# Start of a conditional residual layer: batch 0's input alone, bf16 parts on two engines, row picks dealt out among the first products, beta added first

## The chip, the cores and the metric

The kernel runs on one core of one Trainium2 chip. The core has five engines that work side by side, each through its own instructions in order: TensorE (PE in the profile, its weight loads PEld), VectorE (DVE), ScalarE (ACT), GpSimd (POOL) and SyncE (SP), which here only issues transfers (DMAs). On-chip memory is SBUF, and PSUM for the products of TensorE. Times are device microseconds of one execution; the kernel before took 308.53 us (median of three runs, 308.47 to 308.71).

## The reference

For each of 128 batches (x is [128, 128, 512]: batch, row, column) a language id picks one of 10 small adapters (the setup makes 10 languages; ids are 0 to 8):

```python
w1 = W1[language_ids]                                   # [512, 128] per batch
w2 = W2[language_ids]                                   # [128, 512]
h = relu(einsum('bsh,bha->bsa', x, w1) + b1[language_ids])
adapted = einsum('bsa,bah->bsh', h, w2) + b2[language_ids]
y = x + adapted
normed = (y - mean(y)) * rsqrt(var(y) + 1e-5)           # over the 512 columns
out = x + normed * gamma[language_ids] + beta[language_ids]
```

All of it is float32.

## The kernel before

**Tables.** The rows of beta, gamma and b2 (10 each, 30 in all) are needed on all 128 partitions. They are loaded once as 30 rows (`rows`), split into three bf16 parts whose sum is the float32 value (`parts`, at partitions 0, 32 and 64), and each row is spread by one TensorE product with a column of `pick` (`spread`, L201 to L211): the product selects the three parts of one row, adds them and repeats the sum on all partitions. VectorE or ScalarE copies it from PSUM to one of the tables `beta_b`, `gamma_b`, `b2_b` in SBUF; a row r goes to ScalarE where r % 7 is 1, 3 or 5. `spread_turn(lo, hi)` spreads rows lo to hi - 1: 0 to 9 are beta, 10 to 19 gamma (stored as -gamma/2), 20 to 29 b2. A later use takes the row by a register that holds the batch's language id, so it waits until all ten rows of that table are there. The registers are loaded four batches at a time (`lid`).

**One batch.** TensorE transposes x in four 128x128 pieces (`transpose_x`), ScalarE copies them to SBUF (`copy_xT`); TensorE makes the down product in eight matmuls (`down`), ScalarE adds b1 and applies the relu (`relu`), TensorE makes the up product (`up`). b2 comes in by one of three ways: GpSimd adds the row to x beforehand into a tile r (`add_b2`), VectorE adds it to the product (`vector_b2`), or TensorE adds it as one more bf16 product (inside `up`). The functions `b2_by_matmul` and `b2_by_vector` choose. VectorE then adds the residual and takes row sums (`residual`), ScalarE squares with row sums (`square`) and takes the root, VectorE refines it in three short steps (`rstd`), scales by gamma (`scale`) and writes the result onto the output tile (`finish`). GpSimd has filled that tile with x + beta before (`add_beta`). SyncE stores two batches at a time (`store`).

**Order.** Every instruction is kept in the written order on its engine (`keep`). After the start, a loop over i does for batch i the transposes, for i - 1 the down product, for i - 2 the up product, and for b = i - 3 VectorE's part. In turn b GpSimd adds b2 of batch b + 2, then beta of batch b. There are 5 output tiles of two batches, 4 tiles r, 4 tiles of x (four batches each) and 5 PSUM tiles for products, which the spread rows use too; who fills a tile again waits for its last reader, and a fifth-next output tile so waits for the store of the one before it. Up to batch 8, W1 of a batch is loaded from memory; from 9 on ScalarE copies it out of a table of all ten (`stage_w1`), first `w1e`, loaded at the start in two transfers.

**The start** loads, in SyncE's order: ids, gamma, x of batches 0 and 1, W2 of languages 0 to 2, then W1 of single batches, x two batches at a time, the rest of W2, and `w1e`; ScalarE's queue loads beta, b2, b1. x of batches 10 and 11 is the last of the list, the next four batches of x follow. TensorE first runs `spin`: products of a tile of ones that nothing uses. Then come batches 0 to 3 up to their relu, with the 30 rows spread in between, and the first two up products. The loop begins with i = 3.

**The end.** The last four batches run through `tail`, where GpSimd takes over part of the work of 123, 124 and a quarter of 125 (`by_pool`), and where the stores of 124 and 125 are issued by ScalarE.

Of the kernel before, what the change touches and what calls it, by code (L numbers as in the profile page):

```python
# [8 lines left out]
FP = mybir.dt.float32  # L9
BF = mybir.dt.bfloat16  # L10
I32 = mybir.dt.int32
AF = mybir.ActivationFunctionType
ALU = mybir.AluOpType
ET = mybir.EngineType
PSUM = bass.MemoryType.PSUM

P = 128
# [5 lines left out]
U = 2  # L23
# [3 lines left out]
def cond_resid_kernel(ctx: ExitStack, tc: tile.TileContext, x, itok, W1, b1, W2, b2, gamma, beta, out):  # L27
# [8 lines left out]
    nc = tc.nc  # L36
    B, S, H = x.shape
# [8 lines left out]
    def keep(ins):  # L46

        engine = ins.ins.engine
        if engine in last:
            tc.add_manual_dep(ins.ins, last[engine], behind, reason="kept order")  # L50
        last[engine] = ins.ins.name
        return ins
# [14 lines left out]
    E = B - 5  # L67
# [19 lines left out]
    def load_part(lo, hi):  # L87
        dst = xs[lo // G][:, lo % G : lo % G + hi - lo, :]
        keep(nc.sync.dma_start(out=dst, in_=x[lo:hi].rearrange("b s h -> s b h")))
# [2 lines left out]
    keep(nc.scalar.dma_start(out=rows[0:L, :], in_=beta))  # L92
    keep(nc.sync.dma_start(out=rows[L : 2 * L, :], in_=gamma))
    keep(nc.scalar.dma_start(out=rows[2 * L : 3 * L, :], in_=b2))
    load_part(0, 2)
    keep(nc.scalar.dma_start(out=b1r, in_=b1))

    warm = const.tile([P, 1], FP, name="warm")
# [2 lines left out]
    def load_w1(k):  # L101
        keep(
            nc.sync.dma_start(out=w1[:, :, k, :], in_=W1[:, k * P : (k + 1) * P, :].rearrange("l p a -> p l a"))
        )

    ident = const.tile([P, P], FP, name="ident")
    make_identity(nc, ident)
    eps = const.tile([P, 1], FP, name="eps")
    nc.gpsimd.memset(eps, EPS)
    ones = const.tile([P, P], BF, name="ones")  # L110
    nc.gpsimd.memset(ones, 1.0)

    R = 3 * L
# [64 lines left out]
    load_early(5, L)  # L180
    load_part(2 * G + 2, 3 * G)

    left = rp.tile([P, H], FP, tag="r", name="left")
    keep(nc.vector.tensor_copy(parts[0:R, :], rows[0:R, :]))
    keep(nc.vector.tensor_tensor(left[32 : 32 + R, :], rows[0:R, :], parts[0:R, :], ALU.subtract))
    keep(nc.vector.tensor_copy(parts[32 : 32 + R, :], left[32 : 32 + R, :]))
    keep(nc.vector.tensor_tensor(left[64 : 64 + R, :], left[32 : 32 + R, :], parts[32 : 32 + R, :], ALU.subtract))
    keep(nc.vector.tensor_copy(parts[64 : 64 + R, :], left[64 : 64 + R, :]))

    b1T = const.tile([P, L], FP, name="b1T")  # L190

# [23 lines left out]


    def b2_by_matmul(b):
        return b in (5, B - 1)

    def b2_by_vector(b):  # L220
        return b < 4 or 8 <= b < B - 8 and (b % 4 == 1 if b < 24 else b % 16 in (1, 6, 11) or b % 32 == 30)

    def stage_w1(b):
        w1s[b] = wp.tile([P, KC, A], FP, tag="w1s", name=f"w1s_{b}")
# [22 lines left out]
    def add_beta(b):  # L247
        g, j = divmod(b, 2)
        if j == 0:
            os[g] = op.tile([P, 2, H], FP, tag="o", name=f"o_{g}")  # L250
        v = lid(b, ET.Pool)
        keep(nc.gpsimd.tensor_tensor(os[g][:, j, :], xb(b), beta_b[:, bass.ds(v * H, H)], ALU.add))  # L252

    def down(b):
        phs[b] = p_h.tile([P, P], FP, tag="h", name=f"ph_{b}")
        for k in range(KC):
            keep(
                nc.tensor.matmul(  # L258
                    phs[b], lhsT=w1s[b][:, k, :], rhs=xT[b][:, k, :], start=(k == 0), stop=(k == KC - 1)
                )  # L260
            )
        del xT[b], w1s[b]
# [5 lines left out]
    def up(b):  # L268
        v = lid(b, ET.PE)
        ys[b] = p_y.tile([P, H], FP, tag="y", name=f"py_{b}")  # L270
        m = b2_by_matmul(b)
        if m:
            pick_b = pick[:, bass.ds(v + 2 * L, 1)].to_broadcast([96, P])
            keep(nc.tensor.matmul(ys[b], lhsT=pick_b, rhs=parts[:96, :], start=True, stop=False))
        keep(nc.tensor.matmul(ys[b], lhsT=hT[b], rhs=w2[:, bass.ds(v * H, H)], start=not m, stop=True))  # L275
        del hT[b]
# [203 lines left out]
    def spin(n, width):  # L480
        idle = p_s.tile([P, H], FP, tag="s", name="idle")
        for _ in range(n):
            keep(
                nc.tensor.matmul(
                    idle[:, :width], lhsT=ones, rhs=ones[:, 0:1].to_broadcast([P, width]), start=True, stop=True
                )
            )


    spin(9, H)  # L490
    spin(1, H // 2)

    def spread_turn(lo, hi):
        for r in range(lo, hi):
            spread(r, nc.scalar if r % 7 in (1, 3, 5) else nc.vector)

    def x_turn(b):
        transpose_x(b)
        copy_xT(b)

    x_turn(0)
    transpose_b1()
    spread_turn(0, 4)
    x_turn(1)
    spread_turn(4, 11)
    down(0)
    relu(0)
    spread_turn(11, 15)
    down(1)
    relu(1)  # L510
    x_turn(2)
    spread_turn(15, 19)
    x_turn(3)
    down(2)
    relu(2)
    spread_turn(19, 24)
    down(3)
    relu(3)
    spread_turn(24, R)
    up(0)  # L520
    up(1)

    for i in range(3, B + U):
        b = i - U - 1
        if b > G and b % G == 2 and b // G + 3 < NG:
            load_x(b // G + 3)
        if i == 5:
            load_x(3)
        if i in (8, 10, 12, 14):
            load_w1((i - 8) // 2)  # L530
        if i == 4:
            up(2)
        if i == 5:
            up(3)
        if i > 3 and on(i):
            transpose_x(i)
        if b <= E:
            add_b2(b + 2)
            add_beta(b)
        if i > 4 and on(i - 1):  # L540
            down(i - 1)
        if i > 3 and on(i):
            copy_xT(i)
        if b == 2:
            scalar_means(0)
            deviation(0)
        if i > 4 and on(i - 1):
            relu(i - 1)
        if i + 1 >= LATE and on(i + 1):
            stage_w1(i + 1)  # L550
        if i > 5 and on(i - U):
            up(i - U)


        g, half = divmod(b, 2)
        p = g - 1
        mine, old = 0 <= p < B // 2, 0 <= p - 1 < B // 2
        if b == E:
            add_b2(b + 3)
            add_beta(b + 1)  # L560
            add_b2(b + 4)
            for n in range(b + 2, B):
                add_beta(n)
        if b > E:
            tail(b)
        elif half == 0:
            if on(b):
                vector_b2(b)
                residual(b)
                square(b)  # L570
            if mine:
                scale(2 * p)
                rstd(p, 1)
            if old:
                finish(2 * p - 1)
                store(p - 1)
        else:
            if on(b):
                vector_b2(b)
            if mine:  # L580
                rstd(p, 2)
            if on(b):
                residual(b)
                square(b)
            if mine:
                rstd(p, 3)
                scale(2 * p + 1)
            if mine:
                finish(2 * p)
        if 0 < g and b <= E and half == 1:  # L590
            scalar_means(g)
            deviation(g)
        if FIRST <= i + 1 < LATE:
            stage_w1(i + 1)

        for n, engine in ((i + 3, ET.Activation), (i - U + 3, ET.PE), (b + 1, ET.DVE), (b + 5, ET.Pool)):
            if on(n):
                lid(n, engine)

# [36 lines left out]
```

## Time and profile before

| | |
|---|---|
| runs | 308.47, 308.53, 308.71 us; median 308.53 |
| profiled execution | span 306.5 us from its first to its last instruction; the profile gives no other time for it |
| between span and median | 2.0 us |
| mean time of a beta add, a b2 add on GpSimd (128x512) | 1.395, 1.399 us, one starting each 1.23 us |
| copy of a spread row, VectorE, ScalarE | 0.68, 0.59 us |
| b2 add on VectorE | 0.70 us |
| transfers, mean over the span | 254 GB/s, 77.85 MB |

How to read the rows below. A row of the timeline gives start, duration, engine, line, operation, tiles (out<-in), shapes, how many in a row were merged, and in square brackets the idle time of the engine before it and what ended it. Busy times of merged instructions overlap: an instruction starts up to 0.1 us before the one ahead of it is recorded as ended, so the step from start to start is what one costs. Matmuls are pipelined, and their ends are modelled. A row of the waits gives engine, tile and line, who ended the wait, total, times, longest. A row of the windows gives the stretch, its length, busy time and count of each engine in the order PE, PEld, DVE, ACT, POOL, then the granted clock, the share of the DMA engines and GB/s. SPq and ACTq are the sequencers of those engines, where transfers are issued.

### The profile page before, as it was taken

Reading aid. Unit: us, or ns where it says so; the run is one execution under the profiler, and the core shown is the slowest. Engines: PE = TensorE matmul, PEld = TensorE weight load, DVE = VectorE, ACT = ScalarE, POOL = GpSimd, SP = SyncE. Lnnn points to the kernel's source line nnn. Section 1 sums busy time; section 2 is a strip of 40 time slices with the busy share of each in tenths; the row PEclk is TensorE's granted clock in tenths of the full one; section 3 lists DMA queues with packets and bytes.
Section 4 is the critical chain, followed back from the end, with each engine's and each line's share of the span. In section 5 each row is a group of like instructions: output and inputs, shape, how many; then the busy total and the mean of one; then the engine's idle time right before and its main releaser. Section 6 shows DMA issues by size and latency. Waiting matters only on the chain. (4 is left out here: it accounts for less than half of the span.)

```text
span 306.5 us, 6981 instructions
## 1 busy us (share of the span) xinstructions
PE 294.6 (96%) x1835; PEld 220.0 (72%) x1835; DVE 295.9 (97%) x771; ACT 282.3 (92%) x777; POOL 283.9 (93%) x238
## 2 busy tenths in 40 slices
PE   8999999999999999999999999999999999999960
PEld 3748787777777777777777777777777777777730
DVE  6889999999999999999999999999999999999985
ACT  3858999999999999999999999999999999999981
POOL 1349899999999999999999999999999999999994
PEclk9999999999999999999999999999999999999995
DMA  6999999976678766766777666767776666773324
GB/s 231 379 390 388 373 371 354 387 231 240 221 255 276 250 202 241 226 257 219 259 276 243 213 209 238 265 224 260 275 238 206 226 231 242 246 266 137 135 109 171
DMA packets 43769, 77.85 MB, mean 254 GB/s; under 512 B 1961, under 2 KB 7348, under 8 KB 43730
## 3 DMA queue, kind: packets, MB, share of 16 engines
q1 hardware_dynamic: 43382, 76.84, 72.1%
q10 hardware_dynamic: 348, 0.57, 0.5%
q8 instruction: 15, 0.25, 0.3%
q14 instruction: 24, 0.20, 0.2%
HBM read 43.85 MB, written 33.55 MB: 253 GB/s over the span
## 5 line engine op out<-in xcount | busy, mean ns | idle before, releaser
L252 POOL TENSOR_TENSOR o<-x,beta_b 128x512 f32<-128x512 f32 x128 | 173.9, 1395 | 10.2 <-DVE beta_b L211 9.5
L245 POOL TENSOR_TENSOR r<-x,b_b 128x512 f32<-128x512 f32 x97 | 135.7, 1399 | 7.3 <-DVE b_b L211 6.2
L258 PE MATMUL ph<-xT,w1s 128*128 128x128 f32 x1024 | 135.4, 275 | 0.0
L275 PE MATMUL py<-w,hT 128*128 x256 | 131.2, 595 | 0.5 <-DVE b_b L211 0.5
L258 PEld LDWEIGHTS ph<-xT,w1s 128*128 128x128 f32 x1024 | 124.9, 192 | 1.0 <-ACT hT L266 0.5
L235 PEld LDWEIGHTS pxT<-ident,x 128*128 128x128 f32 x512 | 66.6, 151 | 65.3 <-issue 49.2
L358 DVE SCALAR_TENSOR_TENSOR py<-py,nmean,gamma_b 128x512 f32<-128x512 f32 x126 | 95.0, 754 | 0.9 <-ACT sq L399 0.8
L367 DVE SCALAR_TENSOR_TENSOR o<-py,rstd,o 128x512 f32<-128x512 f32 x122 | 91.2, 748 | 0.0
L315 ACT ACTIVATE sq<-py,sum 128x512 f32<-128x512 f32 x124 | 85.9, 693 | 2.8 <-DVE py L292 2.5
L235 PE MATMUL pxT<-ident,x 128*128 128x128 f32 x512 | 78.2, 276 | 0.0
L239 ACT COPY xT<-pxT 128x512 f32<-128x512 f32 x128 | 74.7, 584 | 3.5 <-PE pxT L235 3.5
L292 DVE SCALAR_TENSOR_TENSOR py<-py,r 128x512 f32<-128x512 f32 x97 | 67.0, 691 | 0.2
L226 ACT COPY w1s<-w 128x512 f32 x107 | 65.5, 612 | 0.0
L266 ACT ACTIVATE hT<-ph,b1T 128x128 f32<-128x128 f32 x128 | 46.9, 366 | 7.9 <-PE ph L258 2.6
L275 PEld LDWEIGHTS py<-w,hT 128*128 128x128 f32 x256 | 39.1, 192 | 2.9 <-issue 1.0
L315 ACT ACTIVATION_READ_ACCUMULATOR sq<-py,sum 128x1 f32 x124 | 25.0, 202 | 0.0
L292 DVE SCALAR_TENSOR_TENSOR py<-py,x 128x512 f32<-128x512 f32 x31 | 21.7, 699 | 0.4
L285 DVE TENSOR_TENSOR py<-py,b_b 128x512 f32<-128x512 f32 x29 | 20.2, 695 | 0.7 <-PE py L275 0.6
L325 ACT ACTIVATE root<-ssq,eps 128x2 f32<-128x2 f32 x62 | 16.4, 265 | 0.0
L292 DVE DVE_READ_ACCUMULATOR py<-py,r 128x1 f32 x97 | 13.7, 141 | 0.0
L306 ACT ACTIVATE nmean<-sum 128x2 f32<-128x2 f32 x62 | 12.3, 198 | 0.0
L329 DVE SCALAR_TENSOR_TENSOR part<-ssq,root 128x2 f32<-128x2 f32 x62 | 9.3, 151 | 0.2 <-ACT root L325 0.2
(55 smaller groups left out, 90.4 us busy)
## 6 DMA issues: line engine op xcount, KB each, us to landing
out_dram<-o SPq DMA_DIRECT2D x61, 512.0 KB, 3.4
x<-in_x_dram SPq DMA_DIRECT2D x29, 1024.0 KB, 6.2
x<-in_x_dram SPq DMA_DIRECT2D x6, 512.0 KB, 8.8
w1e<-in_L_cond_W_dram SPq DMA_DIRECT2D x2, 1280.0 KB, 12.3
w<-in_L_cond_W_dram SPq DMA_DIRECT2D x4, 640.0 KB, 8.1
w1s<-in_L_cond_W_dram SPq DMA_DIRECT2D x9, 256.0 KB, 8.4
w<-in_L_cond_W_dram SPq DMA_DIRECT2D x1, 1792.0 KB, 10.3
w<-in_L_cond_W_dram SPq DMA_DIRECT2D x1, 768.0 KB, 5.4
```

The lines of the kernel that those rows point to most:

```text
L226: keep(nc.scalar.copy(w1s[b].rearrange("p k a -> p (k a)"), src))
L235: keep(nc.tensor.transpose(pxs[b][:, k, :], cols, ident))
L239: keep(nc.scalar.copy(xT[b], pxs.pop(b)))
L245: keep(nc.gpsimd.tensor_tensor(rs[b], xb(b), b2_b[:, bass.ds(v * H, H)], ALU.add))
L252: keep(nc.gpsimd.tensor_tensor(os[g][:, j, :], xb(b), beta_b[:, bass.ds(v * H, H)], ALU.add))
L258: nc.tensor.matmul(phs[b], lhsT=w1s[b][:, k, :], rhs=xT[b][:, k, :], start=(k == 0), stop=(k == KC - 1))
L266: keep(nc.scalar.activation(hT[b], phs.pop(b), AF.Relu, bias=b1T[:, bass.ds(lid(b, ET.Activation), 1)]))
L275: keep(nc.tensor.matmul(ys[b], lhsT=hT[b], rhs=w2[:, bass.ds(v * H, H)], start=not m, stop=True))
L292: nc.vector.scalar_tensor_tensor(ys[b], ys[b], 1.0, r, ALU.mult, ALU.add, accum_out=col(sums, b))
L315: nc.scalar.activation(sq, ys[b], AF.Square, bias=col(sums, b), scale=-float(H), accum_out=col(ssqs, b))
L358: nc.vector.scalar_tensor_tensor(ys[b], ys[b], col(nmeans, b), gamma_b[:, bass.ds(v * H, H)], ALU.add, ALU.mult)
L367: nc.vector.scalar_tensor_tensor(o, ys.pop(b), rstds[g][:, j : j + 1], o, ALU.mult, ALU.add)
```

## The change

Five things change, all but one in the start.

- x of batches 0 and 1 is loaded as two transfers instead of one.
- The tile of ones is filled before the identity matrix; the spin ahead of the first transposes is six products of 512 columns instead of nine and one of 256, and one more product follows b1's transpose.
- The bf16 parts are taken by reading the upper half of each float32 (a view of every second bf16) instead of by casts. VectorE makes two subtractions, ScalarE two copies; the third part is written by the second subtraction. The tile `left` is gone.
- The rows are spread in smaller turns among the first products (5, 3, 3, 3, 3, 3, 4 and 6 rows instead of 4, 7, 4, 4, 5 and 6), and batch 2's transposes come before the second down product.
- GpSimd adds beta of batches 0 to 3 as soon as the beta rows are spread, and in turn b it adds b2, then beta, both of batch b + 2. For batches 0 to 3, b2 is added by GpSimd (0, 2) and TensorE (1, 3) instead of VectorE. GpSimd's ids are loaded one batch further ahead.

```diff
-    load_part(0, 2)
+    load_part(0, 1)
+    load_part(1, 2)
...
+    ones = const.tile([P, P], BF, name="ones")
+    nc.gpsimd.memset(ones, 1.0)
     ident = const.tile([P, P], FP, name="ident")
     make_identity(nc, ident)
     eps = const.tile([P, 1], FP, name="eps")
     nc.gpsimd.memset(eps, EPS)
-    ones = const.tile([P, P], BF, name="ones")
-    nc.gpsimd.memset(ones, 1.0)
...
-    left = rp.tile([P, H], FP, tag="r", name="left")
-    keep(nc.vector.tensor_copy(parts[0:R, :], rows[0:R, :]))
-    keep(nc.vector.tensor_tensor(left[32 : 32 + R, :], rows[0:R, :], parts[0:R, :], ALU.subtract))
-    keep(nc.vector.tensor_copy(parts[32 : 32 + R, :], left[32 : 32 + R, :]))
-    keep(nc.vector.tensor_tensor(left[64 : 64 + R, :], left[32 : 32 + R, :], parts[32 : 32 + R, :], ALU.subtract))
-    keep(nc.vector.tensor_copy(parts[64 : 64 + R, :], left[64 : 64 + R, :]))
+    def upper(lo):
+
+        return rows[lo : lo + R, :].bitcast(BF)[:, 1 : 2 * H : 2]
+
+    keep(nc.vector.tensor_tensor(rows[32 : 32 + R, :], rows[0:R, :], upper(0), ALU.subtract))
+    keep(nc.scalar.copy(parts[0:R, :], upper(0)))
+    keep(nc.vector.tensor_tensor(parts[64 : 64 + R, :], rows[32 : 32 + R, :], upper(32), ALU.subtract))
+    keep(nc.scalar.copy(parts[32 : 32 + R, :], upper(32)))
...
     def b2_by_matmul(b):
-        return b in (5, B - 1)
+        return b in (1, 3, 5, B - 1)

     def b2_by_vector(b):
-        return b < 4 or 8 <= b < B - 8 and (b % 4 == 1 if b < 24 else b % 16 in (1, 6, 11) or b % 32 == 30)
+        return 8 <= b < B - 8 and (b % 4 == 1 if b < 24 else b % 16 in (1, 6, 11) or b % 32 == 30)
...
-    spin(9, H)
-    spin(1, H // 2)
+    spin(6, H)
...
     x_turn(0)
     transpose_b1()
-    spread_turn(0, 4)
+    spin(1, H)
+    spread_turn(0, 5)
     x_turn(1)
-    spread_turn(4, 11)
+    spread_turn(5, 8)
     down(0)
     relu(0)
-    spread_turn(11, 15)
+    spread_turn(8, 11)
+    x_turn(2)
+    for n in range(4):
+        add_beta(n)
+    spread_turn(11, 14)
     down(1)
     relu(1)
-    x_turn(2)
-    spread_turn(15, 19)
+    spread_turn(14, 17)
     x_turn(3)
+    spread_turn(17, 20)
     down(2)
     relu(2)
-    spread_turn(19, 24)
+    spread_turn(20, 24)
     down(3)
     relu(3)
     spread_turn(24, R)
+    add_b2(0)
     up(0)
     up(1)
...
         if b <= E:
             add_b2(b + 2)
-            add_beta(b)
+            if 4 <= b + 2 <= E:
+                add_beta(b + 2)
...
-        for n, engine in ((i + 3, ET.Activation), (i - U + 3, ET.PE), (b + 1, ET.DVE), (b + 5, ET.Pool)):
+        for n, engine in ((i + 3, ET.Activation), (i - U + 3, ET.PE), (b + 1, ET.DVE), (b + 6, ET.Pool)):
```

E is 123, the batch whose turn hands over to the tail.

## The prediction

> **What bounds the kernel now.** I read the page first: its busy shares say which engines could be the bound.
>
> ```profile
> PE 294.6 (96%) x1835; PEld 220.0 (72%) x1835; DVE 295.9 (97%) x771; ACT 282.3 (92%) x777; POOL 283.9 (93%) x238
> ```
>
> Four engines are nearly full, so the shares decide nothing; what matters is where each can still wait. The list of waits, for GpSimd (POOL; microseconds, times, longest):
>
> ```profile
> POOL o L252 <- DVE beta_b L211: 9.5, 1, 9.5
> POOL r L245 <- DVE b_b L211: 6.2, 1, 6.2
> POOL r L245 <- DMA x<-in_x_dram: 1.1, 1, 1.1
> POOL o L252 <- DMA out_dram<-o: 0.5, 1, 0.5
> ```
>
> All its waits lie early: for the spread rows (until 10.98, and 13.48 to 19.67), then for an x load and for a store. From about 52 us it runs to the end without a gap, an add every 1.23 us. TensorE, from 24.5 us on, also runs without a gap, 2.22 and later 2.19 us per batch.
>
> Third, the windows, because the early waits name transfers. The columns after the counts in brackets are granted clock, DMA share and GB/s.
>
> ```profile
> 23.00:33.00 10.00, 10.00 (x69) 8.45 (x69) 9.83 (x27) 8.82 (x26) 9.03 (x8) 1.00 1.05 386
> 43.00:53.00 10.00, 10.00 (x68) 8.11 (x68) 10.00 (x29) 9.70 (x27) 9.35 (x9) 1.00 1.07 355
> ```
>
> The DMA engines are full, and they stay so until about 62 us. Up to there a transfer lands by the bytes in front of it, not by when it is issued. The timeline shows whom that holds. GpSimd:
>
> ```profile
> 33.17 1.28 POOL L245 TENSOR_TENSOR r<-x,b_b 128x512 f32<-128x512 f32 x1 [1.14 <-DMA x<-in_x_dram]
> ...
> 43.19 1.27 POOL L252 TENSOR_TENSOR o<-x,beta_b 128x512 f32<-128x512 f32 x1
> ...
> 50.59 1.30 POOL L245 TENSOR_TENSOR r<-x,b_b 128x512 f32<-128x512 f32 x1
> 52.43 1.27 POOL L252 TENSOR_TENSOR o<-x,beta_b 128x512 f32<-128x512 f32 x1 [0.54 <-DMA out_dram<-o]
> ```
>
> These are the b2 add of batch 10 (waits for x of 10 and 11), the beta adds of 12 and 16 and, between, the b2 add of 18. Beta of 16 needs the output buffer that the store of batches 6 and 7 frees, and waits for that store. TensorE at the same place:
>
> ```profile
> 32.94 1.02 PE L275 MATMUL py<-w,hT 128*128 x2
> 33.80 0.63 PE L235 MATMUL pxT<-ident,x 128*128 128x128 f32 x4
> ```
>
> The second line transposes batch 10: it starts 0.63 us after GpSimd was released by the very load that it needs. Then the start, TensorE and VectorE (DVE):
>
> ```profile
> 1.19 4.45 PE L484 MATMUL idle<-ones 128*128 128x512 bf16 x10 [1.19 <-POOL ones L111]
> ...
> 6.58 1.04 PE L206 MATMUL row<-parts,pick 96*128 96x512 bf16 x4
> ...
> 17.01 1.48 PE L206 MATMUL row<-parts,pick 96*128 96x512 bf16 x6
> ```
>
> ```profile
> 3.13 0.41 DVE L184 CAST parts<-rows 30x512 bf16<-30x512 f32 x1 [0.33 <-DMA rows<-in_L_cond_b_dram]
> ...
> 5.46 0.42 DVE L188 CAST parts<-left 30x512 bf16<-30x512 f32 x1
> ```
>
> The reader sees a start of 18.3 us in which TensorE hardly idles, and parts ready at 5.88. Last the end, GpSimd, then the time to landing of the last stores:
>
> ```profile
> 291.43 5.13 POOL L252 TENSOR_TENSOR o<-x,beta_b 128x512 f32<-128x512 f32 x4
> ...
> 300.43 1.68 POOL L417 TENSOR_TENSOR o<-n,o 128x512 f32<-128x512 f32 x2
> ```
>
> ```profile
> DMA to landing us min/median/max: 2.0/2.0/2.3
> ```
>
> Two chains end here. VectorE's: last piece done at 303.04, its store issued at 303.1, landed 2.3 later at 305.4. GpSimd's: done at 302.10, ScalarE (ACT) issues that store at 302.2; it lands at 304.2 to 304.5 by these durations, 304.7 by the semaphore marks of the trace. So GpSimd's chain has a cover of 0.7 to 1.2 us.
>
> The sum goes against this execution: span 306.5. The median, 308.53, is 2.0 more, which lies outside the span and is kept.
>
> **The change part by part.**
>
> *x of batch 0 alone.* One more SP issue, 0.41 (the 2-batch issue's row). SP issues W2 from 1.96 to 2.43 and then waits for the language ids until 3.55, so 1.1 us of waiting hide it; without that cover the first W1 would land 0.4 later, still ahead of its use. At the 210 to 354 GB/s of the windows from 2 to 6 us, 0.26 MB less is 0.7 to 1.2 us: x of batch 0 is there at about 4.2 instead of by 5.1.
>
> *Ones first, shorter spin.* Spin starts at 1.0 (memset 0.75 + 0.20); six at 0.43 end at 3.6. Batch 0's transposes start at 4.2, four at the 0.21 of this stage, then b1 (0.2), one spin (0.43): first row pick at about 5.7 against 6.58, so −0.9.
>
> *bf16 parts.* Out: three casts of 0.42 on VectorE. In: two copies on ScalarE. VectorE ends at 3.13 + 2 × 0.70 = 4.5. A ScalarE copy of 30x512 is bounded by its rows of 128x128 (0.37) and 128x512 (0.61); I take 0.59, the same length. ScalarE is free at 3.61: ready at 4.8. The subtraction that reads every second bf16 is not in the trace: between a cast's 0.42 and two passes, 1.36; 0.68 taken. At the upper end, parts come at about 6.0 and the first pick 0.3 later than I say; at the lower, nothing moves. ScalarE's copies lie in its idle 2.9 us before 6.52; behind them waits only batch 0's transposed copy.
>
> *Row picks dealt finely.* No pick is removed. TensorE's work from first pick to last is 30 × 0.22 + 4 × 0.89 + 3 × 0.47 = 11.6 us, and the start took 11.75. Finer dealing can win 0.2 there. First picks at the slow pace (0.43) may cost 0.6 of the 0.9. Last pick's end: 17.5 to 17.8 instead of 18.33, last copy (now 19.53) 18.2 to 18.6.
>
> *b2 of batches 0 to 3.* VectorE loses four adds of 0.70 (−2.8). TensorE gains two products of 0.22 (batches 1, 3), GpSimd two adds of 1.23 (0, 2).
>
> *TensorE up to batch 10.* 33.80 − 0.9 (first pick) + 0.44 − 0.46 (the wait before the first up product, for row copies) = 32.9, or 33.4 with slow picks. But x of 10 and 11 lands where it did, behind the same bytes: not before 33.17, the instant GpSimd was released. So **TensorE gains at most 0.63**, whatever the start gives. ScalarE says the same: its copy of W1 for batch 9 (32.20) needs the W1 load that lies 0.52 MB ahead of that x, 1.4 us at 386 GB/s, so about 31.7. With TensorE full from there on, its end and VectorE's end are 0.4 to 0.63 earlier; I take 0.6.
>
> *GpSimd: beta first.* Four beta adds now fill the old idle time (10 to 15 us): free. Afterwards beta of n follows b2 of n, where it followed b2 of n+2. At 52.43 the gate is unchanged, the store of 6 and 7. Before, b2 was done up to 18 by then; now b2 of 18 stands behind beta of 16 and 17. What remains is the same beta adds and **one b2 add more: +1.23**. That the adds reach this gate: b2 of 10 at 33.17, then beta of 10 needs the store of 0 and 1, which stands behind 1.0 MB of x; with its own 0.52 MB that is 33.0 + 4.1 = 37.1. Behind that new wait stands b2 of 11, which VectorE's residual needs at 42.6: 3 us to spare. From there beta 10, b2 11, beta 11, b2 12 end at 42.0; beta of 12 waits until 43.19 as now; seven adds on, 51.84; wait until 52.43. So how early the spread ends does not reach GpSimd's end at all. If the windows' small DMA dips (near 47 us, 0.90 and 1.00 share) fill up, the gate moves 0.3 down. The later b2 adds lead their residual by less: by 5.0 to 7.6 us now, 3.7 less with the new order and 0.6 less with TensorE's gain; the least, batch 124, keeps about 0.1 to 0.3. VectorE need not wait.
>
> *Smaller.* POOL loads ids one batch further ahead (0.32 on its sequencer), beside running adds: nothing.
>
> **Sum.** GpSimd's end 302.10 + 1.23 = 303.33, store issued 303.4, landed 305.4 to 305.9. VectorE's end lands at 304.8. So the end moves by 0.0 to +0.5 from 305.4; I take +0.4, by the trace's marks, and 306.9 for the span: **308.9 us**, +0.1%. One measurement of this kernel cannot tell 0.2% (0.6 us) from nothing.
>
> **The rivals.**
> *A, GpSimd is not behind.* If the gate at 52.43 comes at least 0.6 earlier, or GpSimd's tail adds overlap other waits, TensorE's gain shows: −0.6, 307.9. For it: 0.6 us of slack in front of that gate. Against: the same bytes stand in front.
> *B, no cover at the end (slower).* Place: ScalarE's last store. If that landing already ends the span beside VectorE's, the whole add counts: +1.23, 309.8. It decides against me once the cover is under 0.6. For it: the marks give 0.7, my lowest bound. Against: 1.2 by the store rows.
> *C, the array stays slow longer.* Picks before 6.4 run at 0.43. If the pause between the spin and x (3.6 to 4.2) starts the count anew, fast pace comes as long after 4.2 as it now comes after 1.19 (4.9 us): 9.1 instead of 6.4, 1.3 us lost, batch 10's transposes at 34.2, GpSimd still last. At 1.7 lost the end is +0.7, 309.2; if twice that, 310.9. The profile's clock row reads full through the whole start and cannot tell. The Trainium skill (TensorE: Matmul & The Clock Gate, section on what is actually happening) has the array throttled to half speed until a free-running window of about 3.4 us was busy; by that page a pause that spoils one window would cost an estimated 1.7 us, which this trace neither shows nor excludes.
>
> **How the numbers follow.** Forecast 0.42; A 0.20 (mostly just past 0.2% faster); B 0.28; C 0.10, slower. So faster 0.20, same 0.42, slower 0.38. The forecast's own range is 308.5 to 309.1; with A and B it is 307.8 to 309.9, C's worse half left out.
>
> **What would show it.** In the profile after: first pick before 6, last row copy near 18.4; the transposes of batch 10 at about 33.2 with idle time put down to the x load; GpSimd's wait for stores grown from 0.5 to about 4 us, beta of 16 again near 52.4, its last add near 303.3; ACT's last store issue near 303.4. Wrong would be: beta of 16 well before 52 (A), GpSimd's last add in place but the span 1.2 longer (B), picks 0.43 apart past 7 us (C), or VectorE waiting for b2 adds in the middle, which I priced at nothing.

## The result, and the profile after

The changed kernel took 311.20 us (median of four, 310.23 to 311.71), the kernel before 308.60 beside it: ratio 1.0081, 95% interval 1.0060 to 1.0102. It is slower by 2.6 us, outside the predicted range of 307.8 to 309.9. The profiled execution took 311.0 us with a span of 309.2 (306.5 before): 2.7 us to explain.

The page's busy shares of the changed kernel, then rows of its list of waits:

```profile
PE 295.8 (96%) x1834; PEld 220.6 (71%) x1834; DVE 292.6 (95%) x764; ACT 283.3 (92%) x779; POOL 286.5 (93%) x240
```

```profile
POOL o L255 <- DVE beta_b L214: 11.0, 1, 11.0
POOL r L248 <- DVE b_b L214: 3.9, 1, 3.9
...
POOL o L255 <- DMA out_dram<-o: 3.2, 3, 1.2
...
PE pxT L238 <- DMA x<-in_x_dram: 0.9, 2, 0.6
...
PEld ph L261 <- DMA w1s<-in_L_cond_W_dram: 0.6, 1, 0.6
```

The shares are as they were. But transfers now end more of the waits: GpSimd's for stores grew from one of 0.5 us to three of 3.2, and TensorE waits for x and for W1. The windows say which transfers are late. First the kernel before from 4 to 8 us (the last three columns are granted clock, DMA share and GB/s):

```profile
4.00:6.00 2.00, 1.94 (x7) 0.96 (x6) 1.78 (x4) 0.00 (x0) 0.00 (x0) 1.00 1.00 354
6.00:8.00 2.00, 2.00 (x13) 1.26 (x12) 1.16 (x3) 1.36 (x3) 0.00 (x0) 1.00 1.02 380
```

The same windows of the changed kernel:

```profile
4.00:6.00 2.00, 1.69 (x7) 1.09 (x8) 0.82 (x2) 1.26 (x3) 0.00 (x0) 1.00 0.79 173
6.00:8.00 2.00, 2.00 (x6) 0.78 (x5) 1.22 (x2) 0.72 (x3) 0.00 (x0) 1.00 0.90 268
```

And its later windows, which the prediction showed of before:

```profile
23.00:33.00 10.00, 10.00 (x63) 7.97 (x62) 8.30 (x25) 8.12 (x23) 10.00 (x9) 1.00 1.05 387
43.00:53.00 10.00, 10.00 (x65) 7.89 (x65) 10.00 (x27) 9.71 (x30) 8.91 (x8) 1.00 1.06 341
```

From 4 to 8 us the kernel before moved 2 x (354 + 380) kB = 1.47 MB, the changed one 2 x (173 + 268) = 0.88 MB. The missing 0.59 MB is 1.5 us at 387 GB/s. In this stretch most packets of 2 KB still took 0.084 us, but of the 431 that began here 22 took 0.3 us or more, up to 1.39 us (2 of 715 before, up to 0.36). So parts of the loads fell behind. A load of this size leaves sixteen completion marks in the trace; those of W2's first three languages run from 6.74 to 9.25, where before they ran from 6.80 to 7.35. Afterwards the engines are as full as before, and so nothing is made up. By the trace's semaphore marks W1 of batch 0 landed at 9.94 (8.02 before), x of batches 2 and 3 at 11.97 (10.03), x of 10 and 11 at 34.45 (33.03), and the store of batches 6 and 7 ended at 54.20 (52.36). That last delay is 0.4 us more than that of x of 10 and 11, so not all of it comes from the first 8 us.

The chain that ended last, in order of time (start, duration, what), has one of these on it:

```profile
4.53 7.44 DMA x<-in_x_dram
12.11 0.72 PE pxT L238 x4
```

That is x of batches 2 and 3, from issue to landing. The chain then follows TensorE up to 284.6 us. But behind 54.26 GpSimd waits for nothing, so its own end is counted from there. TensorE's timeline, the start and batch 10:

```profile
1.01 2.74 PE L487 MATMUL idle<-ones 128*128 128x512 bf16 x6 [1.01 <-POOL ones L108]
4.31 1.10 PE L238 MATMUL pxT<-ident,x 128*128 128x128 f32 x4 [0.56 <-DMA x<-in_x_dram]
...
5.94 2.34 PE L209 MATMUL row<-parts,pick 96*128 96x512 bf16 x5
...
12.11 0.72 PE L238 MATMUL pxT<-ident,x 128*128 128x128 f32 x4 [0.32 <-DMA x<-in_x_dram]
...
18.62 1.47 PE L209 MATMUL row<-parts,pick 96*128 96x512 bf16 x6
...
35.69 0.63 PE L238 MATMUL pxT<-ident,x 128*128 128x128 f32 x4
```

The first pick is 0.64 us earlier than before, and the last six are 1.61 us later (17.01). Batch 10's transposes are 1.89 us later (33.80), and this distance then stays: TensorE is full, so what is lost at the start is lost at the end. VectorE follows TensorE; its last pieces start 1.85 us later.

GpSimd's timeline in the changed kernel, at its three waits for stores:

```profile
38.57 1.27 POOL L255 TENSOR_TENSOR o<-x,beta_b 128x512 f32<-128x512 f32 x1 [1.22 <-DMA out_dram<-o]
...
44.64 2.52 POOL L255 TENSOR_TENSOR o<-x,beta_b 128x512 f32<-128x512 f32 x2 [1.09 <-DMA out_dram<-o]
...
54.26 2.52 POOL L255 TENSOR_TENSOR o<-x,beta_b 128x512 f32<-128x512 f32 x2 [0.93 <-DMA out_dram<-o]
```

And at the end:

```profile
294.72 5.04 POOL L255 TENSOR_TENSOR o<-x,beta_b 128x512 f32<-128x512 f32 x4
...
303.63 1.68 POOL L420 TENSOR_TENSOR o<-n,o 128x512 f32<-128x512 f32 x2
```

Beta of 16 comes 1.83 us later (52.43 before), and GpSimd ends at 305.31, 3.20 later: 1.83 from the gate, 1.37 behind it.

### The profile page after: what moved, and what is told of

It is laid out like the page before. It is cut to its first block, busy times and chain, and to the rows that moved or that the text cites. A ratio compares the mean times of both kernels' runs of the same rounds, so it can differ in the third digit from the quotient of the medians.

```text
span 309.2 us, 7001 instructions
## 1 busy us (share of the span) xinstructions
PE 295.8 (96%) x1834; PEld 220.6 (71%) x1834; DVE 292.6 (95%) x764; ACT 283.3 (92%) x779; POOL 286.5 (93%) x240
## 4 chain that ended last, share of the span: by engine, by line
PE 88%; POOL 5%; DMA 2%; DVE 2%; SPq 1%; issue 1%; POOLq 0%; DVEq 0%
PE ph L261 35%; PE py L278 34%; PE pxT L238 18%; DMA x<-in_x_dram 2%; POOL o L255 2%; POOL r L248 1%; PE row L209 1%; POOL n L418 1%; DVE py L361 1%; POOL o L420 1%; DVE b_b L214 0%; POOLq L640 0%; DVE py L295 0%; SPq L155 0%; SPq L89 0%
## 5 line engine op out<-in xcount | busy, mean ns | idle before, releaser
L255 POOL TENSOR_TENSOR o<-x,beta_b 128x512 f32<-128x512 f32 x128 | 163.3, 1290 | 14.2 <-DVE beta_b L214 11.0
L248 POOL TENSOR_TENSOR r<-x,b_b 128x512 f32<-128x512 f32 x99 | 127.4, 1290 | 3.9 <-DVE b_b L214 3.9
L295 DVE SCALAR_TENSOR_TENSOR py<-py,r 128x512 f32<-128x512 f32 x99 | 68.3, 690 | 2.0 <-POOL r L248 1.6
L295 DVE SCALAR_TENSOR_TENSOR py<-py,x 128x512 f32<-128x512 f32 x29 | 20.3, 700 | 0.3
L288 DVE TENSOR_TENSOR py<-py,b_b 128x512 f32<-128x512 f32 x25 | 17.2, 690 | 0.1
```

What stands on the lines that cost most here:

```text
L248: keep(nc.gpsimd.tensor_tensor(rs[b], xb(b), b2_b[:, bass.ds(v * H, H)], ALU.add))
L295: nc.vector.scalar_tensor_tensor(ys[b], ys[b], 1.0, r, ALU.mult, ALU.add, accum_out=col(sums, b))
```

## The experiments

All runs at a glance. "TensorE" is batch 20's transposes against the kernel before; "gate" is the start of beta of 16; the next column is the time from there to the end of GpSimd's last add. These three and the span are of the profiled execution; median and ratio are of the timed runs, the ratio to the kernel before on the same chip.

| kernel | median us | ratio, 95% interval | span | TensorE | gate | gate to end |
|---|---|---|---|---|---|---|
| before | 308.53 | | 306.5 | 0 | 52.43 | 249.68 |
| changed | 311.20 | 1.0081 (1.0060 to 1.0102) | 309.2 | +1.89 | 54.26 | 251.05 |
| e1 changed, again | 311.47 | 1.0097 (1.0074 to 1.0119) | 309.8 | +3.15 | 54.68 | 250.96 |
| e2 x pair restored | 310.04 | 1.0049 (1.0026 to 1.0072) | 308.6 | +1.25 | 53.58 | 250.88 |
| e3 long spin | 310.64 | 1.0072 (1.0053 to 1.0092) | 308.9 | +1.61 | 53.93 | 250.85 |
| e4 beta behind b2 of n+2 | 310.04 | 1.0052 (1.0029 to 1.0075) | 308.1 | +1.64 | 54.23 | 249.65 |
| e5 before, x split | 309.80 | 1.0040 (1.0025 to 1.0055) | 307.0 | +0.46 | 53.15 | 249.65 |
| e6 before, GpSimd's order | 309.33 | 1.0014 (0.9999 to 1.0028) | 307.6 | -0.47 | 52.98 | 251.02 |
| e7 e2 + e3 + e4 | 308.67 | 0.9996 (0.9983 to 1.0009) | 306.8 | -0.07 | 52.75 | 249.83 |
| e8 changed, x of 1 later | 309.66 | 1.0033 (1.0019 to 1.0047) | 307.6 | +1.19 | 52.09 | 251.06 |
| e9 e8, spin, e4 | 309.03 | 1.0017 (1.0001 to 1.0033) | 307.0 | +0.52 | 53.10 | 249.75 |
| e10 before, x of 1 later | 309.15 | 1.0024 (1.0005 to 1.0044) | 307.8 | +0.60 | 54.04 | 249.75 |
| e11 before, two queues | 308.35 | 0.9990 (0.9977 to 1.0002) | 306.7 | +0.23 | 52.87 | 249.60 |
| e12 before, row halves | 310.20 | 1.0055 (1.0036 to 1.0074) | 308.3 | +2.02 | 53.63 | 249.82 |
| e13 changed, two queues | 310.89 | 1.0074 (1.0048 to 1.0100) | 309.9 | +3.44 | 54.34 | 250.91 |
| e14 e13, spin, e4 | 309.77 | 1.0039 (1.0010 to 1.0067) | 308.9 | +2.70 | 54.24 | 249.89 |
| e15 e14, b1 first | 308.40 | 0.9995 (0.9986 to 1.0004) | 306.6 | +0.10 | 52.69 | 249.76 |

The last column falls into two groups. Wherever GpSimd has the new order it is 250.85 to 251.06, wherever it has the old one 249.60 to 249.89, whatever else is changed. That is the one b2 add (1.23 us) of the prediction.

**e1, the changed kernel once more.** No edit. Is the slow start chance?

> The changed kernel once more, to see whether what its profile shows is there each time. In the profiled execution the 2 KB packets between 4.5 and 8 us took 0.4 to 1.4 us instead of 0.08, W2's first three languages landed at 9.25 (before 7.35), and every later transfer of the start came 1.4 to 1.9 late; the picks ran at 0.43 until about 9; GpSimd's beta of 16 began at 54.26 (before 52.43). Theory D (slow transfers come with the change): again 115 to 270 GB/s from 4.5 to 7, beta of 16 at 54.0 or later, 310 to 312 us. Rival N (a disturbance of that one execution): the early transfers run at 360 GB/s or more, beta of 16 near 52.5, about 309.2 us.

It is not chance: 205 and 312 GB/s in the two windows from 4 to 8 us, beta of 16 at 54.68, 311.47 us. But another thing differed, in TensorE's timeline:

```profile
5.47 1.25 PE L209 MATMUL row<-parts,pick 96*128 96x512 bf16 x5
...
9.94 1.16 PE L261 MATMUL ph<-xT,w1s 128*128 128x128 f32 x8 [2.10 <-DMA w1s<-in_L_cond_W_dram]
```

The same program ran its picks 0.22 apart here and 0.43 apart above. The fast picks won nothing: TensorE then stood 2.10 us for W1 of batch 0.

**e2, the x pair in one load again.**

```diff
-    load_part(0, 1)
-    load_part(1, 2)
+    load_part(0, 2)
```

> x of batches 0 and 1 in one transfer again, all else as changed. Theory D1 (the split x brings the slow transfers): 360 GB/s or more from 4.5 on, W2's first part landed by 7.5, beta of 16 at 52.4 to 52.6, GpSimd's last add 1.8 earlier than in the changed kernel, 309.0 to 309.5 us. Rival D2 (the split has no part in it): slow packets as in the changed kernel, beta of 16 at 54 or later, within 0.5 us of the changed kernel.

The early transfers were back at 343 and 382 GB/s, W1 of batch 0 landed at 7.99, and 1.2 us of the 2.6 were gone. (The intervals of e2 and of the changed kernel overlap; e5 and e8 below are clearer.) Still there were GpSimd's add and slow picks, behind a pause of 1.45 us. TensorE's timeline of e2:

```profile
5.20 1.10 PE L237 MATMUL pxT<-ident,x 128*128 128x128 f32 x4 [1.45 <-DMA x<-in_x_dram]
...
6.83 2.23 PE L208 MATMUL row<-parts,pick 96*128 96x512 bf16 x5
```

But beta of 16 did not come back to 52.4 to 52.6, nor the time to 309.0 to 309.5: the gate is at 53.58. VectorE finished batch 7 at 44.53 (43.27 before), the store of 6 and 7 was issued at 44.82 (44.35) and was under way for 8.7 us (8.0). Around 48 us some transfers are slow again; the windows from 47 to 50 us, of the kernel before, the changed one and e2:

```profile
47.00:50.00 3.00, 3.00 (x21) 2.40 (x20) 3.00 (x8) 2.86 (x7) 3.00 (x3) 1.00 0.98 326
47.00:50.00 3.00, 3.00 (x23) 2.53 (x22) 3.00 (x9) 3.00 (x11) 3.00 (x4) 1.00 1.03 302
47.00:50.00 3.00, 3.00 (x22) 2.46 (x21) 3.00 (x10) 2.85 (x10) 3.00 (x4) 1.00 0.97 293
```

**e3, the long spin again.**

```diff
-    spin(6, H)
+    spin(9, H)
+    spin(1, H // 2)
...
-    spin(1, H)
     spread_turn(0, 5)
```

> The spin of before (nine and a half products ahead of the first transposes, none after b1), all else as changed. Theory C (the shorter spin keeps the array slow): picks 0.22 apart from the first one, the last pick at about 18.0 instead of 19.7, the transposes of batch 10 1.5 us earlier. Theory G (GpSimd sets the end by the store gates): the time moves by less than 0.4 us all the same. Rival P (TensorE's late start sets the end): 1.5 us faster, 309.5 us or less.

TensorE's timeline of e3:

```profile
5.72 1.25 PE L209 MATMUL row<-parts,pick 96*128 96x512 bf16 x5
...
9.72 1.16 PE L261 MATMUL ph<-xT,w1s 128*128 128x128 f32 x8 [1.63 <-DMA w1s<-in_L_cond_W_dram]
```

Fast picks again, and again the gain ended in a wait for W1: batch 10's transposes came 0.27 us earlier than in the changed kernel, not 1.5. e3 is 0.6 and 0.8 us below the two medians of the changed kernel (311.20, 311.47), more than the 0.4 of theory G and far from the 1.5 of rival P. With transfers this late the slow array is not the main cause of the loss.

**e4, beta of n behind b2 of n+2 again.**

```diff
-            if 4 <= b + 2 <= E:
-                add_beta(b + 2)
+            if b >= 4:
+                add_beta(b)
```

> In the loop beta of batch b again behind b2 of batch b + 2 (batches 0 to 3 still first), all else as changed. Theory G (the new order costs GpSimd one add at the gate of the store of 6 and 7): its last add ends 1.2 earlier than in the changed kernel, and the end falls to what TensorE's chain gives, 0.8 to 1.2 us faster, about 310.2 us. Rival P: TensorE's chain already sets the end, and the time stays within 0.3 us.

The timeline of e4, the last rows of GpSimd and of VectorE:

```profile
302.20 1.68 POOL L420 TENSOR_TENSOR o<-n,o 128x512 f32<-128x512 f32 x2
...
303.80 0.88 DVE L427 SCALAR_TENSOR_TENSOR o<-py,rstd,o 128x256 f32<-128x256 f32 x2
```

GpSimd is done at 303.88 instead of 305.31, with the gate where it was (54.23); now VectorE's chain, 1.63 late, sets the end, and the span falls by 1.1.

**e5, the split alone, in the kernel before.** The reverse of e2's edit, on the kernel before.

> The kernel before with one edit: the first x load, of batches 0 and 1 together, is split into two loads of one batch each. Nothing else is changed. Theory D (the split itself slows the transfers that follow it): between 4 and 8 us the transfers run at 115 to 300 GB/s as in the changed kernel, W1 of batch 0 lands at 9.7 to 9.9 (8.02 before), beta of 16 starts at 53.8 to 54.3 (52.43 before), TensorE and GpSimd end 1.4 to 1.9 later, and the time is 310.0 to 310.5. Rival N (the split is harmless alone, it needs the earlier picks or copies beside it): the early throughput is that of before, 290 to 405 GB/s, beta of 16 starts at 52.4 to 52.6, and the time is 308.0 to 308.7.

The windows of e5:

```profile
4.00:6.00 2.00, 1.94 (x9) 0.88 (x7) 1.71 (x4) 0.00 (x0) 0.00 (x0) 1.00 0.69 203
6.00:8.00 2.00, 2.00 (x13) 1.35 (x13) 1.56 (x4) 1.80 (x4) 0.00 (x0) 1.00 0.93 289
```

The split is enough to slow the transfers: W1 of batch 0 at 9.86, 309.80 us, 1.1 us slower. That is a little less than expected, and so are the delays in the profile, 0.72 us for beta of 16 and 0.46 for TensorE where 1.4 to 1.9 were expected; the profiled execution was the fastest of the ten (308.74). In the kernel before the down product of batch 0 comes behind 11 picks, and its wait for W1 was 0.64:

```profile
9.90 1.16 PE L259 MATMUL ph<-xT,w1s 128*128 128x128 f32 x8 [0.64 <-DMA w1s<-in_L_cond_W_dram]
```

**e6, GpSimd's order alone, in the kernel before.**

```diff
+    for n in range(4):
+        add_beta(n)
     spread_turn(15, 19)
...
             add_b2(b + 2)
-            add_beta(b)
+            if 4 <= b + 2 <= E:
+                add_beta(b + 2)
...
-        for n, engine in ((i + 3, ET.Activation), (i - U + 3, ET.PE), (b + 1, ET.DVE), (b + 5, ET.Pool)):
+        for n, engine in ((i + 3, ET.Activation), (i - U + 3, ET.PE), (b + 1, ET.DVE), (b + 6, ET.Pool)):
```

> The kernel before with GpSimd's new order alone: beta of 0 to 3 among the first products, then beta of n behind b2 of n; x, the bf16 parts, the picks, the spin and the choice of b2 engines stay as before. Theory G (one b2 add more behind the gate): beta of 16 again at 52.4 to 52.6, GpSimd's last two adds 1.23 later, done at 303.3 instead of 302.1, TensorE and VectorE where they were before; the end moves by 0 to 0.5, time 308.6 to 309.1 if the last stores have the cover that I gave them, 309.8 if they have none. Rival H (the add is regained, or the order has no part in the loss): GpSimd's end within 0.3 of 302.1 and 308.4 to 308.7.

GpSimd's timeline of e6:

```profile
43.29 2.52 POOL L252 TENSOR_TENSOR o<-x,beta_b 128x512 f32<-128x512 f32 x2 [1.07 <-DMA out_dram<-o]
...
52.98 2.51 POOL L252 TENSOR_TENSOR o<-x,beta_b 128x512 f32<-128x512 f32 x2 [0.99 <-DMA out_dram<-o]
...
302.33 1.67 POOL L417 TENSOR_TENSOR o<-n,o 128x512 f32<-128x512 f32 x2
```

Gates 0.10 and 0.55 later than before, the end of GpSimd 1.89 later, 1.34 of it behind the gate; the span grew by 1.1, so the cover at the end was 0.8. 309.33 us, 0.6 above the kernel before; the interval of the ratio just reaches down to no change.

**e7, all three undone** (the edits of e2, e3 and e4 together). What stays is the new bf16 parts, the fine dealing, b2 of 0 to 3 off VectorE and the four early betas.

> The changed kernel with three of its parts undone: x of 0 and 1 in one load, the spin of 9 and a half ahead of x (none behind b1), and in the loop beta of n behind b2 of n+2. What stays is bf16 parts on two engines, fine dealing, b2 of 0 to 3 off VectorE, and beta of 0 to 3 early. If transfers, slow picks and the order are the whole loss, all three are gone: early throughput as before, picks 0.22 apart, beta of 16 at 52.4 to 52.7, GpSimd's end within 0.3 of 302.1, TensorE 0 to 0.6 ahead of before, time 307.9 to 308.7. If the finer dealing itself costs something (down of batch 0 put ahead of its load, TensorE held there), TensorE is 0.3 to 1.2 late from then on and the time is 308.9 to 309.8.

308.67 us beside 308.74: the three are the whole loss, and what stays is worth nothing that can be measured.

**e8, x of batch 1 later.** Split, but not back to back.

```diff
-    load_part(1, 2)
...
     load_first(0)
+    load_part(1, 2)
     load_first(1)
```

> The changed kernel with x of batch 1 issued behind W1 of batch 0 instead of right behind x of batch 0; all else as changed. It asks whether it is the two small loads back to back that slow the packets. If it is (theory back-to-back): W2 of 0 to 2 lands near 7.3, W1 of batch 0 at 7.7 to 8.2, 2 KB packets near 0.1 us throughout, beta of 16 at 52.4 to 53.6, and the time 309.3 to 309.9 (what is left is the GpSimd add and the slow picks). If the slow packets come with any start in which x of batch 0 goes alone: 115 to 300 GB/s again between 4 and 8 us, beta of 16 at 53.9 to 54.7, and 310.5 to 311.5.

The windows of e8:

```profile
4.00:6.00 2.00, 1.64 (x7) 1.04 (x8) 0.68 (x2) 1.21 (x3) 0.00 (x0) 1.00 1.00 364
6.00:8.00 2.00, 2.00 (x6) 0.60 (x4) 1.17 (x2) 0.72 (x3) 0.00 (x0) 1.00 1.05 396
```

Full throughput, W1 of batch 0 at 7.23, beta of 16 at 52.09. x of batch 0 alone does no harm to the transfers. What is left of the loss, 0.9 us, is the add behind the gate and slow picks (TensorE +1.19).

**e9, e8 with a spin of 8 and e4's order.**

```diff
-    spin(6, H)
+    spin(8, H)
```

> The changed kernel with three edits: x of batch 1 issued behind W1 of batch 0, the spin ahead of x 8 wide products in place of 6 (so that it ends at 4.4, no pause before x of batch 0), and in the loop beta of n behind b2 of n+2. If the transfers, the slow picks and the order are the whole loss and the earlier x is worth something once they are gone: picks 0.22 apart from about 5.9, last pick's end near 17.6, beta of 16 at 52.0 to 52.4, GpSimd done at 301.7 to 302.1, TensorE 0.3 to 0.6 ahead of before, time 307.9 to 308.4. If the early x is worth nothing even so (the opening is bound by W1 loads and by TensorE's own work): TensorE within 0.2 of before, 308.5 to 308.9.

TensorE's timeline of e9:

```profile
5.64 1.25 PE L209 MATMUL row<-parts,pick 96*128 96x512 bf16 x5
8.08 0.72 PE L238 MATMUL pxT<-ident,x 128*128 128x128 f32 x4 [1.19 <-DMA x<-in_x_dram]
```

Both expectations missed: 309.03. Picks were fast, and then TensorE waited 1.19 us for x of batch 1, which now landed behind W2 and W1.

**e10, the same later load in the kernel before** (e8's edit alone).

> The kernel before with one edit: x of batch 0 alone first, x of batch 1 behind W1 of batch 0. Spin, parts, picks and GpSimd as before. Theory back-to-back (the loss of the split comes from two small x loads one behind the other): no stretch under 280 GB/s between 3 and 8 us, W1 of batch 0 lands at 7.2 to 7.7, beta of 16 at 52.0 to 52.5, time 308.1 to 308.8. Rival (any start in which x of batch 0 goes alone loses DMA time): a stretch under 200 GB/s, W1 of batch 0 later than 9, time 309.5 to 310.2.

309.15, above what the first theory gave, and the rival did not hold either: 341 and 400 GB/s, W1 of batch 0 at 7.19. TensorE again stood for batch 1's transposes until 8.00. The gate of the profiled execution was late (54.04) beside the slow stretch that e2 showed: 268 GB/s from 47 to 50 us, with 18 packets of 0.36 to 1.37 us that began between 47.5 and 50.1. The kernel before shows eight such there (0.58 at most); what brings them was not tried.

**e11, two queues.** In the kernel before:

```diff
-    load_part(0, 2)
+    load_part(0, 1)
+    keep(nc.scalar.dma_start(out=x_0[:, 1:2, :], in_=x[1:2].rearrange("b s h -> s b h")))
```

> The kernel before with x of batches 0 and 1 as two loads, the second issued by ScalarE's queue instead of SP's. It asks whether the slow packets need both loads in one queue. If they do: throughput of 280 GB/s and more from 3.5 us on, W1 of batch 0 lands near 8.0, and 308.4 to 308.9. If it is W2 going behind two small loads, whatever queue they are in: under 200 GB/s somewhere between 4 and 6 us, W1 of batch 0 at 9.5 to 9.9, and 309.5 to 310.2.

The windows of e11:

```profile
4.00:6.00 2.00, 1.94 (x7) 0.97 (x6) 1.72 (x4) 0.00 (x0) 0.00 (x0) 1.00 1.02 335
6.00:8.00 2.00, 2.00 (x11) 1.11 (x10) 0.93 (x3) 1.14 (x3) 0.00 (x0) 1.00 1.05 406
```

Same bytes and sizes, issued within 0.2 us of the same moment, but one of the two loads in ScalarE's queue: 335 and 406 GB/s where e5 had 203 and 289, and 308.35 us where e5 had 309.80. One thing more differs: with one load less ahead of it on SP, W2 is issued at 1.91 (2.38 in e5). The Trainium skill ("DMA: Bandwidth & Descriptors", section "Issuing engines are not separate DMA queues") says that transfers started from several engines run on the same 16 DMA engines and that this saves only issue time. e5 against e11 does not fit that: 0.47 us of issue time was saved, the ratios are 1.0040 and 0.9990 with their intervals apart, 1.3 us against the kernel before beside each, and the measurement decides.

**e12, the pair cut by rows.** In the kernel before, two loads of rows 0 to 63 and 64 to 127 of both batches:

```diff
-    load_part(0, 2)
+    for lo in (0, P // 2):
+        keep(nc.sync.dma_start(out=x_0[lo : lo + P // 2, 0:2, :], in_=x[0:2, lo : lo + P // 2].rearrange("b s h -> s b h")))
```

> The kernel before with its load of x of 0 and 1 cut the other way: rows 0 to 63 of both batches, then rows 64 to 127 of both; two loads of the same size one behind the other, as in the change, but each with both batches. If two small loads back to back are enough for the slow packets: under 200 GB/s somewhere between 4 and 6 us, W1 of batch 0 at 9.5 to 9.9, 309.5 to 310.2. If it is the order of the batches (all rows of one, then all rows of the other): throughput as before, W1 of batch 0 near 8.0, 308.4 to 308.9.

The windows of e12:

```profile
4.00:6.00 2.00, 1.58 (x4) 0.30 (x2) 1.76 (x4) 0.00 (x0) 0.00 (x0) 1.00 1.02 223
6.00:8.00 2.00, 1.65 (x7) 1.04 (x8) 0.17 (x1) 0.51 (x1) 0.00 (x0) 1.00 0.92 287
```

Slow again, 310.20, as expected if two loads of 0.26 MB back to back in SP's queue are enough. But this does not rule out the order of the batches, because more than the order is new here: each load fills half the partitions, W2 is issued at 2.91 and the first W1 at 4.31 (2.38 and 3.60 in e5). And its slow stretch looks different: of the 498 packets that began from 4 to 8 us, 175 took 0.115 to 0.2 us and none more than 0.5 (e5: 14 of 480, up to 0.78), and W2's first completion mark comes at 7.76, where in e5 it comes at 6.79, as before, and only the last are late.

**e13, two queues in the changed kernel** (e11's edit on the changed kernel).

> The changed kernel with one edit: x of batch 1 is issued by ScalarE's queue instead of SP's. If the one-queue pair is what slows the transfers: 260 GB/s and more from 3.5 us on, W1 of batch 0 lands at 7.5 to 8.0 (9.94 in the changed kernel), beta of 16 at 52.4 to 53.2, and what stays is the order (GpSimd done at 303.3 to 304.1) and perhaps slow picks (TensorE 0 to 1.2 late): time 309.2 to 309.9. If the slow transfers come back in the changed kernel for another reason: W1 of batch 0 after 9.4, beta of 16 after 53.8, 310.5 to 311.5.

310.89, in the range of the second account, but not for its reason. The early transfers were good (300 and 407 GB/s, W1 of batch 0 at 7.77), and neither account had foreseen the next wait: b1 now stood behind x of batch 1 in ScalarE's queue, and TensorE waited 2.05 us for it.

**e14, e13 with a spin of 8 and e4's order.**

> The changed kernel with three edits: x of batch 1 from ScalarE's queue, the spin ahead of x 8 wide products in place of 6, and in the loop beta of n behind b2 of n+2. If the earlier x of batch 0 is worth something once the three losses are gone: first pick near 5.7, picks 0.22 apart, down of batch 0 at 7.9 to 8.6, TensorE 0.4 to 0.9 ahead of before, GpSimd done at 301.8 to 302.5, time 307.7 to 308.2. If it is worth nothing (TensorE held by the loads of W1 and x again): TensorE within 0.3 of before and 308.3 to 308.8.

TensorE's timeline of e14:

```profile
7.24 0.23 PE L197 MATMUL b1p<-ident,b1r 10*128 10x10 f32 x1 [2.37 <-DMA b1r<-in_L_cond_b_dram]
```

309.77, with single times in two groups, 308.1 to 309.0 and 310.6 to 312.0; the profile is of the upper group and shows the wait for b1, 2.37 us, and picks at 0.43 behind it. Neither expectation held.

**e15, e14 with b1 issued ahead of x of batch 1.**

```diff
+    keep(nc.scalar.dma_start(out=b1r, in_=b1))
     keep(nc.scalar.dma_start(out=x_0[:, 1:2, :], in_=x[1:2].rearrange("b s h -> s b h")))
-    keep(nc.scalar.dma_start(out=b1r, in_=b1))
```

> The kernel of e14 (changed kernel, x of batch 1 from ScalarE's queue, spin of 8 ahead of x, beta of n behind b2 of n+2) with the load of b1 issued ahead of x of batch 1 on ScalarE's queue. If the wait for b1 was all that was left: b1's transpose right behind batch 0's transposes, at about 5.0, first pick near 5.5 to 5.8, down of batch 0 at 7.9 to 8.6, TensorE 0.2 to 0.7 ahead of before, time 307.8 to 308.4. If the earlier start is then lost on another load: TensorE waits for W1 or x before batch 3, TensorE within 0.3 of before or later, 308.4 to 309.2.

TensorE's timeline of e15:

```profile
5.63 1.24 PE L209 MATMUL row<-parts,pick 96*128 96x512 bf16 x5
7.17 0.72 PE L238 MATMUL pxT<-ident,x 128*128 128x128 f32 x4 [0.29 <-DMA x<-in_x_dram]
...
10.32 0.72 PE L238 MATMUL pxT<-ident,x 128*128 128x128 f32 x4 [0.23 <-DMA x<-in_x_dram]
```

308.40, on the border of the two ranges; TensorE at +0.10 is the second's. With all three losses gone the first pick is 0.95 us earlier than before and the down product of batch 0 1.16 earlier. But 0.66 of that is three picks that now come behind it, and 0.23 goes into the second wait for x, so the first up product is only 0.18 earlier; the two b2 products of batches 1 and 3 (0.22 each) would turn that into 0.26 later, and 0.10 is left at batch 10. No version tried beats the kernel before by more than can be measured: e7, e11 and e15 are level with it.

## Why the prediction was wrong

**The step that failed** is in the parts on TensorE and on GpSimd: "x of 10 and 11 lands where it did, behind the same bytes", and from it "At 52.43 the gate is unchanged". The bytes were the same; the time that they took was not: x of 10 and 11 landed 1.42 us later, and the gate came 1.83 later. I priced the split at an issue of 0.41 us (hidden, rightly: the first W1 was issued at 3.59 against 3.55) and at fewer bytes ahead of batch 0, and took the throughput from the windows of before as given. Splitting cost 0.59 MB of throughput between 4 and 8 us (0.48 in e5). e5 shows it in the kernel before; e2, e7, e8, e11 and e15 show the throughput back once the two loads are not back to back in one queue. All other transfers up to 62 us inherit it, which the prediction's own reading, a queue that is always full, would have given at once.

The split is not the whole loss. Undone, it gives back 1.2 us of 2.6 (e2); alone, it costs 1.1 (e5). In e2 the gate is still 1.15 us late and TensorE 1.25, which the prediction did not have either: "TensorE gains at most 0.63" priced slow picks at 0.6 of the 0.9 won, but the five first picks alone took 2.14 us in the changed kernel where five fast ones take 1.08 (e1). The prediction also held the gate by the early bytes alone; in e2 it came late beside a late VectorE and the slow stretch near 48 us, and how much each of the two adds stays open.

**x of batch 0 alone, and the parts: right.** x landed at 4.17 (4.2 foreseen), the parts were ready at 4.73 (4.8), and the two prices that no row had shown came out as taken, in VectorE's and ScalarE's timelines:

```profile
3.97 0.68 DVE L190 TENSOR_TENSOR parts<-rows 30x512 bf16<-30x512 f32 x1
```

```profile
4.11 0.62 ACT L191 COPY parts<-rows 30x512 bf16<-30x512 bf16 x1
```

**First pick, 5.7 foreseen, 5.94 measured; last copy wrong.** The last row copy ended at 21.14, not 18.2 to 18.6. "Finer dealing can win 0.2" left out what the dealing moves: the down product of batch 0 went from behind 11 picks to behind 8, and batch 2's transposes ahead of batch 1's down product, so both meet their loads sooner. With transfers on time that is harmless (e7); with late ones it turned fast picks into the waits of e1 and e3.

**GpSimd: one add more, right, and its gate wrong.** The 1.23 us stand in all seven kernels with the new order (1.17 to 1.38 more than in the kernel before), and e4 takes them out. The waits for stores grew from 0.5 to 3.2 (4 foreseen).

**The cover at the end: somewhat too large.** Where GpSimd ends last, the span ends 3.6 to 4.1 us behind its last add (e6 3.6, changed 3.9, e2 and e3 4.1); the kernel before has 4.4. That is a cover of 0.3 to 0.8 where 0.7 to 1.2 was given. The 2.7 us are then 1.83 for the gate and 1.37 behind it, less 0.5 of cover.

**The rivals.** A did not occur. B (no cover, 309.8) is not what happened, though its direction was right. C named a slow pace, and it came, in the profiled execution until about 9 us; but it does not carry the loss of the changed kernel: e1 and e3 had fast picks in their profiles and took 311.47 and 310.64 us. (From 1.19 to 6.4 are 5.2 us, not the 4.9 that C took; its 9.1 would be 9.4.) Its price shows only where transfers are on time: from e2 to e7 TensorE comes from +1.25 to -0.07, and there the picks are fast, while beta's order, the other edit between them, is no work of TensorE's.

**One effect unforeseen and free:** VectorE waits 1.44 us (at 22.59) for GpSimd's b2 add of batch 0, which was its own before. e7 has the same wait and no loss.

## What to carry to other kernels

Where the DMA queues stay full for tens of microseconds, a change to the first transfers is a change to all of them: price it in bytes per microsecond of the windows that follow, not by its issue time. A start that is split for one engine's sake needs its other small loads looked at in the same way, since each experiment that cured one wait met the next load in line (W1, x of batch 1, b1). And an add that moves from ahead of a wait for a buffer to behind it could be counted here: it cost about its length behind the gate, wherever the gate was.

## What the runs showed of the hardware

Two loads of 0.26 MB one behind the other in SP's queue, with W2 behind them, came with lower throughput for about 4 us. In the six kernels that had them (changed, e1, e3, e4, e5 and, with row halves, e12) the windows read 173 to 265 GB/s from 4 to 6 us and 268 to 312 from 6 to 8; in the eleven others 300 to 364 and 349 to 407. One load of both, other loads in between, or the second in ScalarE's queue avoids it. Why is open: in the five kernels with whole batches a few 2 KB packets take many times their 0.084 us and W2's last completion marks come at 9.00 to 9.25, though its first come at 6.63 to 6.84, but what the packets wait for is in no view, and other sizes were not tried. One rival was not tested: in the six W2 is issued at 2.38 us or later, in the eleven by 1.96, and no run parts that from the two loads.

The array's pace after a short spin is not fixed. With the spin of 2.74 us and a pause of 0.6, the same program ran picks 0.43 apart in one execution and 0.22 in another (e1); with 3.6 us of spin and more, and no pause behind it, the picks were fast from the first, at 5.6 to 5.7 us (e3, e9, e15). This agrees with the Trainium skill ("TensorE: Matmul & The Clock Gate", section "What's actually happening"), which has a free-running window of about 3.4 us decide. The profile's clock column read 1.00 beside picks at 0.43 in the changed kernel, and 0.50 beside such picks in e14 from 8 to 10 us, after TensorE had stood 2.37 us: it is not to be read as the pace over stretches this short.
